# Two pre-activation 5x5 convolutions: direct products on row quads replaced by minimal F(4,3) filtering on 2x2 pixel blocks

## The chip, the cores and the metric

The kernel runs on one core of a Trainium2 chip. The core has a matrix engine (TensorE, "PE" in the profile, with "PEld" for its weight loads), three engines for elementwise work (VectorE "DVE", ScalarE "ACT", GpSimd "POOL"), and queues from which transfers between DRAM and the on-chip memories are issued; here SyncE ("SP") issues nearly all of them. On-chip data lies in SBUF, 128 partitions wide; TensorE writes its sums to PSUM, which VectorE and ScalarE read and POOL doesn't. The metric is the device time of one execution, in microseconds. The time before is the median of three runs.

## What is computed

Two layers of x = x + conv(groupnorm(x)) on an array of 8 images, 32 channels, 252 x 252 pixels, all in float32. The norm has 16 groups of two channels. The convolution is written with Fourier transforms in the reference; it comes to a 5x5 convolution with padding. The core of the reference:

```python
def conv(x, weight):                      # the same for both layers
    k = weight.shape[-1]; p = k // 2
    xp = jnp.pad(x, ((0, 0), (0, 0), (p, p), (p, p)), mode='reflect')
    ...
    wp = jnp.roll(wp, shift=(-k // 2, -k // 2), axis=(-2, -1))
    x_fft = jnp.fft.fft2(xp)
    w_fft = jnp.fft.fft2(wp)
    out_fft = jnp.einsum('bihw,oihw->bohw', x_fft, w_fft)
    out = jnp.fft.ifft2(out_fft).real
    return out[:, :, p:-p, p:-p]
...
x = x + conv(_gn(x), L0_conv_weight)
x = x + conv(_gn(x), L1_conv_weight)
```

Written out, an output pixel is a sum over 32 input channels and 5 x 5 taps of the reflected, normalised image, where the taps reach from two pixels to one side to three (after the roll) in the padded plane; the padded plane that is needed has 256 x 256 pixels, rows and columns -1 to 254.

## The kernel before

**Layout.** The 128 partitions are four quadrants of 32 channels. A quadrant holds every fourth image row, so one column position on 128 partitions is 32 channels of four neighbouring rows. An output slot is four rows; it needs two neighbouring blocks of four input rows and five column taps, so ten products of 128 x 128 matrices that are banded in (input row, output row). A product is taken for two slots at once, 2 x 252 = 504 columns; `conv` (line 201) issues the products, and an add on VectorE (line 209) puts the result on x, in place. A slot pair at the edge of a chunk splits some products in two of 252 columns.

**Stages.** An image is eight chunks of eight slots. `load` (line 67) brings a chunk of x from DRAM by four transfers, `partial_stats` (line 118) takes mean and variance of two slots at a time, `finish_stats` (lines 124 to 147) joins these, averages over the eight partitions of a group by two tiny products, and takes 1 / sqrt by a table on ScalarE and a Newton step. `normalise` (line 162) writes the normalised, shifted and padded chunk g on VectorE, and ScalarE copies edge rows and columns (lines 174 to 185). `store` (line 72) writes the result. x stays in SBUF through both layers, 18 chunk buffers for two images of eight chunks each; so each image is read once and written once.

**Order.** The program runs image after image and layer after layer; inside, chunk after chunk, each chunk's input normalised one chunk ahead of its products. The second layer of an image can't begin before the first has ended, since its norm needs the whole of the first layer's output. The code names an engine for every operation, and buffers by pools with a count of buffers (three for g, six in PSUM for products). The order on each engine's queue isn't written by hand: a planner in the framework takes the operations in an order that it works out from dependences, free buffers, the program's order and its own costs, and puts in the waits. Each engine then executes its own queue in that order.

The lines of the run that the change replaces:

```python
for b in range(B):
    for l in range(2):
        for c in range(NCH):
            ...
            for j in range(0, slots[c], 2):
                if l == 0 and b + 1 < B:
                    partial_stats(b + 1, 0, c, j)
                conv(b, l, c, j)
                if l == 0:
                    partial_stats(b, 1, c, j)
            if l == 1:
                store(b, c)
```

Of the kernel before, what the change touches and what calls it, by code (L numbers as in the profile page):

```python
# [31 lines left out]
EPS = 1e-5  # L32


@with_exitstack
def tile_conv_preact_x2(ctx: ExitStack, tc: tile.TileContext, x: bass.AP, w0: bass.AP, w1: bass.AP, out: bass.AP):
# [3 lines left out]
    assert (C, K, H % 4) == (32, 5, 0)  # L40
    NSLOT = H // 4
    CH = 8
    NCH = (NSLOT + 1) // CH
    WP = W + 4
    NPAIR = (NSLOT + 1) // 2
    slots = [min(CH, NSLOT - c * CH) for c in range(NCH)]

    const = ctx.enter_context(tc.tile_pool(name="const", bufs=1))
    xpool = ctx.enter_context(tc.tile_pool(name="xpool", bufs=2 * NCH + 2))
    gpool = ctx.enter_context(tc.tile_pool(name="gpool", bufs=3))  # L50
    small = ctx.enter_context(tc.tile_pool(name="small", bufs=3))
    ps_conv = ctx.enter_context(tc.tile_pool(name="ps_conv", bufs=6, space=bass.MemoryType.PSUM))
    ps_stat = ctx.enter_context(tc.tile_pool(name="ps_stat", bufs=2, space=bass.MemoryType.PSUM))

    quads = [slice(q * Q, (q + 1) * Q) for q in range(4)]

    def dram_rows(t: bass.AP, b: int, c: int, q: int):
        rows = t[b].rearrange("ch (t r) w -> r ch t w", r=4)
        return rows[(q - 1) % 4, :, c * CH : c * CH + slots[c], :]

# [1 line left out]
    xt = {}  # L62

    def load(b: int, c: int):
        t = xpool.tile([P, CH, W], F32, tag="x", name=f"x_{b}_{c}")
        for q in range(4):
            nc.sync.dma_start(t[quads[q], : slots[c], :], dram_rows(x, b, c, q))  # L67
        xt[b, c] = t

    def store(b: int, c: int):  # L70
        for q in range(4):
            nc.sync.dma_start(dram_rows(out, b, c, q), xt[b, c][quads[q], : slots[c], :])

    wraw = []
    for l, w in enumerate((w0, w1)):
        t = const.tile([P, K, K, C], F32, tag=f"wraw{l}", name=f"wraw{l}")
        for q in range(4):
            nc.scalar.dma_start(t[quads[q]], w)
        wraw.append(t)
    for b in range(min(2, B)):  # L80
        for c in range(NCH):
            load(b, c)

# [1 line left out]
    wt = []  # L85
    for l in range(2):
        eng = (nc.vector, nc.gpsimd)[l]
        t = const.tile([P, 2, K, 4, C], F32, tag=f"wt{l}", name=f"wt{l}")
        eng.memset(t, 0.0)
        for q in range(4):  # L90
            for blk in range(2):
                for row in range(4):
                    a = row + 4 - 4 * blk - q
                    if 0 <= a < K:
                        eng.tensor_copy(t[quads[q], blk, :, (row + 1) % 4, :], wraw[l][quads[q], a, :, :])  # L95
        wt.append(t.rearrange("p b c q o -> p b c (q o)"))

# [1 line left out]
    ident = const.tile([P, P], F32, tag="ident", name="ident")  # L99
    make_identity(nc, ident)  # L100
    member = const.tile([P, C // 2], F32, tag="member", name="member")
# [10 lines left out]
    stats, norm = {}, {}  # L112

    def partial_stats(b: int, l: int, c: int, j: int):
        if (b, l) not in stats:
            stats[b, l] = small.tile([P, NPAIR, 6], F32, tag="stats", name=f"stats_{b}_{l}")
        n = min(2, slots[c] - j)
        nc.vector.bn_stats(  # L118
            stats[b, l][:, (c * CH + j) // 2, :], xt[b, c][:, j : j + n, :].rearrange("p t w -> p (t w)")
        )  # L120

    def finish_stats(b: int, l: int):
# [24 lines left out]
        nc.vector.tensor_mul(mr[:, 1:2], inv, fix)  # L147
        norm[b, l] = mr

# [116 lines left out]
```

## Time and profile before

| What | Value |
|---|---|
| Median of three runs | 4438.5 us (4436.24 to 4440.49) |
| Span of the profiled execution | 4439.0 us |
| DMA, mean over the span | 30 GB/s, 132.59 MB |
| HBM read, written | 65.85 MB, 65.03 MB |
| VectorE busy | 1375.4 us |
| ScalarE busy | 103.1 us |
| POOL busy | 7.3 us |

The profile is of one execution, and nothing of its time lies outside its span as far as the runs can tell (4439.0 beside 4438.5). The groups of instructions give, for a line of the code and an engine, how often, how long in all, and the mean in nanoseconds; float32 products appear as two records each, and records of products in a row overlap, so the mean of a record isn't the pace. "Idle before" is the time an engine stood still in front of instructions of the group, and the arrow names what ended it.

### The profile page before, as it was taken

The page shows a single profiled execution, that of the slowest core. Times are in us where ns is not written, and L with a number is a line of the kernel's source. Part 1 is how long each engine was busy: PE and PEld are TensorE (multiplying, and loading weights), DVE is VectorE, ACT ScalarE, POOL GpSimd, SP SyncE. Part 2 cuts the span into 40 slices and gives each one's busy share as a digit, 9 for nine tenths or more (in the row PEclk, how much of TensorE's full clock was granted, in tenths as well). Part 3 has the DMA queues.
Part 4 walks back from the last instruction along what each step waited for, and adds up shares of the span by engine and source line. Part 5 has one row for each costly group of instructions (what it writes and reads, how often), then busy time and mean ns, then how long its engine had stood idle before and what let it go on. Part 6 is the DMA issues. An engine that isn't in the chain of part 4 may idle for free.

```text
span 4439.0 us, 26427 instructions
## 1 busy us (share of the span) xinstructions
PE 4296.0 (97%) x11424; PEld 2159.0 (49%) x11424; DVE 1375.4 (31%) x1726; ACT 103.1 (2%) x609; POOL 7.3 (0%) x27
## 2 busy tenths in 40 slices
PE   4999999999999999999999999999999999999999
PEld 2454445444554445444544454454445544554444
DVE  6423332332333233332333323332322332232321
ACT  0000000000000000000000000000000000000000
POOL 0000000000000000000000000000000000000000
PEclk9999999999999999999999999999999999999999
DMA  9001320023100221002210023100320001100011
GB/s 173 0 0 38 65 44 1 0 47 64 36 0 0 56 55 36 0 0 56 55 36 1 0 56 65 27 0 0 66 55 8 0 10 28 28 9 1 10 28 36
DMA packets 137716, 132.59 MB, mean 30 GB/s; under 512 B 8320, under 2 KB 137344, under 8 KB 137600
## 3 DMA queue, kind: packets, MB, share of 16 engines
q1 hardware_dynamic: 137216, 130.09, 13.9%
q8 instruction: 89, 1.46, 0.1%
q10 hardware_dynamic: 384, 0.82, 0.1%
q14 instruction: 27, 0.22, 0.0%
HBM read 65.85 MB, written 65.03 MB: 29 GB/s over the span
## 4 chain that ended last, share of the span: by engine, by line
PE 97%; DVE 2%; DMA 1%; ACT 0%; issue 0%; SPq 0%; ACTq 0%; DVEq 0%
PE ps L201 96%; DVE g L162 1%; DMA x<-in_x_dram 1%; DVE mv L124 0%; PE pv L135 0%; DVE stats L118 0%; DMA wraw<-in_L_conv_weight_dram 0%; DVE x L209 0%; PE pm L127 0%; DVE dev L130 0%; DVE sq L133 0%; DVE sq L132 0%; ACT g L182 0%; DVE mr L128 0%; SPq L67 0%
## 5 line engine op out<-in xcount | busy, mean ns | idle before, releaser
L201 PE MATMUL ps<-g,wt 128*128 128x504 f32 (+1 forms) x11360 | 4282.6, 539 | 54.4 <-ACT g L185 54.4
L201 PEld LDWEIGHTS ps<-g,wt 128*128 128x128 f32 x11360 | 2147.7, 189 | 2186.5 <-issue 2076.2
L209 DVE TENSOR_TENSOR x<-ps,x 128x504 f32<-128x504 f32 (+1 forms) x512 | 345.1, 674 | 2435.6 <-PE ps L201 2432.5
L162 DVE TENSOR_SCALAR g<-x,mr 32x1764 f32<-32x1764 f32 (+4 forms) x496 | 668.7, 1365 | 578.1 <-PE ps L201 571.8
L118 DVE BATCH_NORM_STATS2 stats<-x 128x6 f32<-128x504 f32 (+1 forms) x512 | 325.2, 669 | 26.6 <-DMA x<-in_x_dram 18.7
L182 ACT COPY g<-g 128x8 f32<-128x8 f32 x128 | 26.2, 205 | 2766.5 <-DVE g L162 2734.5
L127 PE MATMUL pm<-mv,avg 128*128 128x1 f32 x32 | 6.4, 270 | 66.5 <-DVE mv L124 66.5
L127 PEld LDWEIGHTS pm<-mv,avg 128*128 128x128 f32 x32 | 5.3, 207 | 69.6 <-DVE mv L124 69.6
L184 ACT COPY g<-g 128x8 f32<-128x8 f32 x128 | 25.6, 200 | 0.0
L185 ACT COPY g<-g 128x8 f32<-128x8 f32 x128 | 25.6, 200 | 0.0
L183 ACT COPY g<-g 128x8 f32<-128x8 f32 x128 | 25.5, 199 | 0.2
L135 PE MATMUL pv<-sq,avg 128*128 128x1 f32 x32 | 8.0, 318 | 15.2 <-DVE sq L133 15.2
L140 ACT ACTIVATE std<-var 128x1 f32<-128x1 f32 x16 | 3.2, 203 | 800.2 <-DVE var L137 800.2
L181 ACT COPY g<-row 32x252 f32<-32x252 f32 x16 | 6.4, 399 | 432.9 <-PE ps L201 432.9
L124 DVE BATCH_NORM_AGGREGATE mv<-stats 128x2 f32<-128x192 f32 x16 | 15.4, 996 | 0.3
L135 PEld LDWEIGHTS pv<-sq,avg 128*128 128x128 f32 x32 | 6.6, 257 | 16.5 <-DVE sq L133 16.5
L174 ACT COPY g<-g 32x252 f32<-32x252 f32 x16 | 6.4, 401 | 204.2 <-DVE g L162 204.2
L179 ACT COPY g<-g 32x252 f32<-32x252 f32 x16 | 6.4, 401 | 28.3 <-DVE g L162 28.3
L180 ACT COPY g<-g 32x252 f32<-32x252 f32 x16 | 6.4, 400 | 0.2
L176 ACT COPY row<-g 32x252 f32<-32x252 f32 x16 | 6.4, 397 | 0.4
L95 DVE COPY wt<-wraw 32x160 f32<-32x160 f32 x20 | 4.9, 302 | 2.6 <-DMA wraw<-in_L_conv_weight_dram 2.6
L95 POOL COPY wt<-wraw 32x160 f32<-32x160 f32 x20 | 5.5, 315 | 5.5 <-DMA wraw<-in_L_conv_weight_dram 5.3
(21 smaller groups left out, 30.6 us busy)
## 6 DMA issues: line engine op xcount, KB each, us to landing
x<-in_x_dram SPq DMA_DIRECT2D x224, 252.0 KB, 5.2
out_dram<-x SPq DMA_DIRECT2D x224, 252.0 KB, 4.2
x<-in_x_dram SPq DMA_DIRECT2D x32, 220.5 KB, 4.6
out_dram<-x SPq DMA_DIRECT2D x32, 220.5 KB, 3.5
wraw<-in_L_conv_weight_dram ACTq DMA_DIRECT2D x8, 100.0 KB, 5.1
```

The costliest lines, as they stand in the source:

```text
L95: eng.tensor_copy(t[quads[q], blk, :, (row + 1) % 4, :], wraw[l][quads[q], a, :, :])
L118: nc.vector.bn_stats(stats[b, l][:, (c * CH + j) // 2, :], xt[b, c][:, j : j + n, :].rearrange("p t w -> p (t w)"))
L124: nc.vector.bn_aggr(mv, stats.pop((b, l)).rearrange("p n s -> p (n s)"))
L127: nc.tensor.matmul(pm, avg, mv[:, 0:1], start=True, stop=True)
L135: nc.tensor.matmul(pv, avg, sq, start=True, stop=True)
L162: nc.vector.tensor_scalar(g[rows, dst, 1 : W + 1], src, mr[rows, 0:1], mr[rows, 1:2], ALU.subtract, ALU.mult)
L182: nc.scalar.copy(g[:, :, 0:1], g[:, :, 2:3])
L183: nc.scalar.copy(g[:, :, W + 1 : W + 2], g[:, :, W - 1 : W])
L184: nc.scalar.copy(g[:, :, W + 2 : W + 3], g[:, :, W - 2 : W - 1])
L185: nc.scalar.copy(g[:, :, W + 3 : W + 4], g[:, :, 3:4])
L201: nc.tensor.matmul(ps[:, at : at + m, :], wt[l][:, blk, kc, :], g[:, lo : lo + m, K - 1 - kc : K - 1 - kc + W], start=(i == 0), stop=(i == ...
L209: nc.vector.tensor_add(xs, ps[:, :n, :], xs)
```

## The change

The kernel is rewritten in its layout, its arithmetic, its storage between the layers and its order.

- **Blocks.** The partitions hold 2 x 2 pixel blocks: four quadrants for column parity and row parity. The padded plane becomes 128 x 128 blocks. A 5 x 5 kernel on pixels is a 3 x 3 kernel on blocks.
- **F(4,3) along block rows.** Four block rows of output are made from six transformed inputs instead of from 4 x 3 row taps: `transform` forms six sums v0 to v5 of input rows, `conv` multiplies each by three matrices (one per block column) for four such sets at once, 4 x 126 = 504 columns, and ten VectorE operations unite the six results into four rows. The matrices u are combinations of the kernel's rows (`make_matrices`).
- **Residual in the matrices.** x itself is no longer added: `own_pixel` adds (standard deviation) x identity, transformed in the same way, to the middle matrix of each of the six, per image and layer; the mean is added by ScalarE's copy of the first product.
- **Layer 1 through DRAM.** x isn't kept in SBUF. Its statistics are taken from a load of their own (`input_stats`), a second load brings the blocks for the convolution, layer 1's output goes to a DRAM scratch array in block layout with its padding (`to_scratch`), and layer 2 loads it from there and normalises it in place. `to_output` interleaves the columns on ScalarE and stores.
- **Normalise** is on ScalarE; the pad columns and two of the transform's subtractions are on POOL.
- **Order.** A step is a group of 16 block rows, eight per image and layer. Phases (image, layer) alternate between two images: (0,1) (1,1) (0,2) (2,1) (1,2) ... (7,1) (6,2) (7,2), counting images from 0 and layers from 1. Input statistics of the next image are taken during the phase before its first layer. Each step's input is transformed one step ahead of its products and loaded two ahead.

The core of the diff (new code; what it replaces is printed above):

```diff
+    def input_stats(b: int, c: int):
+        n = min(8, 63 - 8 * c)
+        t = spool.tile([P, 8, W], F32, tag="sx", name=f"sx_{b}_{c}")
+        rows = x[b].rearrange("ch (t r) w -> r ch t w", r=4)
+        for q in range(4):
+            nc.sync.dma_start(t[quads[q], :n], rows[q, :, 8 * c : 8 * c + n, :])
+        for j in range(0, n, 2):
+            m = min(2, n - j)
+            nc.vector.bn_stats(stat_slot(b, 0, 4 * c + j // 2), t[:, j : j + m, :].rearrange("p t w -> p (t w)"))
...
+    def own_pixel(b: int, l: int):
+        mr = norm[b, l]
+        for pc in range(2):
+            h = halves[pc]
+            nc.vector.scalar_tensor_tensor(
+                ut[l][h, :, 1 + pc, h], own[h], mr[h, 3:4], ubase[l][h], ALU.mult, ALU.add
+            )
...
+    def load(b: int, l: int, T: int):
+        nr = min(GR + 2, PB - GR * T)
+        if l:
+            g = gpool.tile([P, GR + 2, PB], F32, tag="g", name=f"g_{b}_{l}_{T}")
+            nc.sync.dma_start(g[:, :nr, :], scratch[b][:, GR * T : GR * T + nr, :])
...
+        t = xpool.tile([64, GR + 2, W], F32, tag="x", name=f"x_{b}_{T}")
...
     def normalise(b: int, l: int, T: int):
+        if T == 0:
             finish_stats(b, l)
         mr = norm[b, l]
+        nr = min(GR + 2, PB - GR * T)
+        if l:
+            g = gt[b, l, T][:, :nr, :].rearrange("p r k -> p (r k)")
+            nc.scalar.activation(g, g, AF.Identity, bias=mr[:, 2:3], scale=mr[:, 1:2])
+            return
...
+        for pc in range(2):
+            for pr in range(2):
+                q = quad(pc, pr)
+                nc.scalar.activation(
+                    g[q, :nr, 1 - pc : 1 - pc + NB],
+                    t[quads[pr], :nr, 1 - pc : W : 2],
+                    AF.Identity,
+                    bias=mr[q, 2:3],
+                    scale=mr[q, 1:2],
+                )
+        for dst, src in ((0, 1), (127, 125)):
+            nc.gpsimd.tensor_copy(g[halves[0], :nr, dst : dst + 1], g[halves[0], :nr, src : src + 1])
...
+    def transform(b: int, l: int, T: int):
...
+        nc.vector.scalar_tensor_tensor(
+            flat,
+            g[:, 0:GR, :].rearrange("p r k -> p (r k)"),
+            -4.0,
+            g[:, 2 : GR + 2, :].rearrange("p r k -> p (r k)"),
+            ALU.mult,
+            ALU.add,
+        )
+        c = apool.tile([P, NT, 2, PB], F32, tag="c", name=f"c_{n}")
+        cf = c.rearrange("p t r k -> p t (r k)")
+        nc.gpsimd.tensor_sub(cf, rows_of(g, 3), rows_of(g, 1))
+        v05 = vpool.tile([P, NT, 2, PB], F32, tag="v05", name=f"v05_{n}")
+        nc.gpsimd.tensor_sub(
+            v05.rearrange("p t r k -> p t (r k)"),
+            ab[:, :, 2:4, :].rearrange("p t r k -> p t (r k)"),
+            ab[:, :, 0:2, :].rearrange("p t r k -> p t (r k)"),
+        )
+        v = [vpool.tile([P, NT, PB], F32, tag=f"v{k}", name=f"v{k}_{n}") for k in range(1, 5)]
+        nc.vector.tensor_add(v[0], ab[:, :, 2, :], ab[:, :, 1, :])
+        nc.vector.tensor_sub(v[1], ab[:, :, 2, :], ab[:, :, 1, :])
+        nc.vector.scalar_tensor_tensor(v[2], c[:, :, 0, :], 2.0, c[:, :, 1, :], ALU.mult, ALU.add)
+        nc.vector.scalar_tensor_tensor(v[3], c[:, :, 0, :], -2.0, c[:, :, 1, :], ALU.mult, ALU.add)
...
+    def conv(b: int, l: int, T: int):
...
+        def product(f: int):
+            ps = ps_conv.tile([P, NT, NB], F32, tag="m", name=f"m{f}_{n}")
+            for b3 in range(3):
+                nc.tensor.matmul(
+                    ps,
+                    ut[l][:, f, b3, :],
+                    vs[f][:, :, 2 - b3 : 2 - b3 + NB],
+                    start=(b3 == 0),
+                    stop=(b3 == 2),
+                )
+            return ps
...
+        m1 = product(1)
+        a1 = temp("a1")
+        nc.scalar.activation(a1, m1, AF.Identity, bias=mr[:, 0:1])
+        m2 = product(2)
+        s1, d1 = temp("s1"), temp("d1")
+        v.tensor_add(s1, m2, a1)
+        v.tensor_sub(d1, a1, m2)
+        m3 = product(3)
+        a3 = temp("a3")
+        nc.scalar.copy(a3, m3)
+        m4 = product(4)
+        s2, d2 = temp("s2"), temp("d2")
+        v.tensor_add(s2, m4, a3)
+        v.tensor_sub(d2, a3, m4)
+        v.scalar_tensor_tensor(yo[1], d2, 2.0, d1, ALU.mult, ALU.add)
+        v.scalar_tensor_tensor(yo[2], s2, 4.0, s1, ALU.mult, ALU.add)
+        m0 = product(0)
+        v.tensor_add(s1, m0, s1)
+        v.tensor_add(yo[0], s1, s2)
+        m5 = product(5)
+        v.tensor_add(d1, m5, d1)
+        v.scalar_tensor_tensor(yo[3], d2, 8.0, d1, ALU.mult, ALU.add)
...
+    for i, (b, l, T) in enumerate(steps):
+        prefetch(i + 1 + AHEAD)
+        if (b, l) in before:
+            input_stats(before[b, l], T)
+        if i + 1 < len(steps):
+            normalise(*steps[i + 1])
+            transform(*steps[i + 1])
+            if steps[i + 1][2] == 0 and steps[i + 1][1] != l:
+                own_pixel(*steps[i + 1][:2])
+        conv(b, l, T)
+        if i + 1 < len(steps) and steps[i + 1][2] == 0 and steps[i + 1][1] == l:
+            own_pixel(*steps[i + 1][:2])
```

The new pools have two buffers each for the x tiles, the statistics' tiles, g, the transformed inputs v, the row tile y and the output tile o, one for the transform's intermediates (`ab`, `c`), and seven in PSUM for products.

More of the change, by code (lines that the diff above doesn't have):

```diff
@@ L32 @@
 EPS = 1e-5
+NB = 126
+PB = 128
+TR = 4
+NT = 4
+GR = TR * NT
+NG = PB // GR
+NF = 6
 @with_exitstack
@@ L39, in tile_conv_preact_x2 @@
     K = w0.shape[1]
[L40 to L46, printed above, removed]
[L48 to L50 removed]
+    assert (C, K, H, W) == (32, 5, 252, 252)
+    const = ctx.enter_context(tc.tile_pool(name="const", bufs=1))
@@ L55, in tile_conv_preact_x2 @@
+    ps_stat = ctx.enter_context(tc.tile_pool(name="ps_stat", bufs=1, space=bass.MemoryType.PSUM))
     quads = [slice(q * Q, (q + 1) * Q) for q in range(4)]
[L57 to L96, printed above, removed]
+    halves = [slice(0, 64), slice(64, 128)]
@@ new lines, in tile_conv_preact_x2, with prefetch @@
+    taps = [load_taps(0, w0)]
+    for c in range(NG):
+        input_stats(0, c)
+    make_own()
+    make_matrices(0, taps[0])
+    make_matrices(1, load_taps(1, w1))
+    phases = [(0, 0)]
+    for b in range(1, B):
+        phases += [(b, 0), (b - 1, 1)]
+    phases.append((B - 1, 1))
+    steps = [(b, l, T) for b, l in phases for T in range(NG)]
+    AHEAD = 2
+    loaded = 0
+    def prefetch(upto: int):
+        nonlocal loaded
+        while loaded < min(upto, len(steps)):
+            load(*steps[loaded])
+            loaded += 1
@@ new lines, in tile_conv_preact_x2 @@
+    prefetch(AHEAD)
+    before = {}
+    for i, (b, l) in enumerate(phases):
+        if l == 0 and i:
+            before[phases[i - 1]] = b
+    normalise(*steps[0])
+    transform(*steps[0])
+    own_pixel(*steps[0][:2])
+    for i, (b, l, T) in enumerate(steps):
[10 more added lines that the diff above has]
+            own_pixel(*steps[i + 1][:2])
```

257 lines of the change are left out of this document (174 added, 83 removed).

## The prediction

> **What bounds the kernel now.** I read the page's busy shares first, then its chain of work that ended last, then the groups of instructions.
>
> ```profile
> span 4439.0 us, 26427 instructions
> PE 4296.0 (97%) x11424; PEld 2159.0 (49%) x11424; DVE 1375.4 (31%) x1726; ACT 103.1 (2%) x609; POOL 7.3 (0%) x27
> ...
> L201 PE MATMUL ps<-g,wt 128*128 128x504 f32 (+1 forms) x11360 | 4282.6, 539 | 54.4 <-ACT g L185 54.4
> ```
>
> PE is busy for 97% of the span and stands idle in front of its products for 54.4 us in all. No other engine is busy for a third. Only fewer or faster products can shorten this, until another engine is the bound. So I need the price of a product, and then what every other engine is given per product. The trace records each float32 product twice; the pace is read from the VectorE adds that close a group of ten products (timeline of VectorE):
>
> ```profile
> 385.06 0.68 DVE L209 TENSOR_TENSOR x<-ps,x 128x504 f32<-128x504 f32 x1 [2.97 <-PE ps L201]
> 393.51 0.68 DVE L209 TENSOR_TENSOR x<-ps,x 128x504 f32<-128x504 f32 x1 [7.77 <-PE ps L201]
> ```
>
> Ten products of 504 columns take 393.51 - 385.06 = 8.45 us, 0.845 us each.
>
> **Is the order the program's?** It decides whether waits add up. Early timeline of VectorE, and a later row:
>
> ```profile
> 63.58 2.42 DVE L118 BATCH_NORM_STATS2 stats<-x 128x6 f32<-128x504 f32 x4
> 66.02 5.11 DVE L162 TENSOR_SCALAR g<-x,mr 64x2016 f32<-64x2016 f32 x4
> 71.05 0.66 DVE L209 TENSOR_TENSOR x<-ps,x 128x504 f32<-128x504 f32 x1
> ...
> 329.52 1.90 DVE L124 BATCH_NORM_AGGREGATE mv<-stats 128x2 f32<-128x192 f32 x2
> ```
>
> The program puts chunk 2's normalise (L162) behind all four adds of chunk 0; VectorE runs it ahead of the first. At 329.52 two images' statistics are closed together, though the program asks for the second one a whole convolution later. So each queue's order is a planner's, which fills idle time with later work as buffers allow. I take it to do the same with the new code.
>
> **The change, step by step.** A step is one group of 16 block rows (32 image rows) of one image and layer; there are 8 x 2 x 8 = 128.
>
> TensorE: 6 transformed inputs x 3 block columns = 18 products of 504 columns, 18 x 0.845 = 15.2 us a step, 1947 us in all, against 4282.6 now.
>
> VectorE gets most of what is added. Its prices, from the groups by form:
>
> ```profile
> L209 DVE TENSOR_TENSOR x<-ps,x 128x504 f32<-128x504 f32 x496 | 338.4, 682 | 2384.3 <-PE ps L201 2381.2
> L209 DVE TENSOR_TENSOR x<-ps,x 128x252 f32<-128x252 f32 x16 | 6.7, 420 | 51.4 <-PE ps L201 51.4
> ...
> L182 ACT COPY g<-g 128x8 f32<-128x8 f32 x128 | 26.2, 205 | 2766.5 <-DVE g L162 2734.5 <-DVE inv L142 32.0
> ...
> L174 ACT COPY g<-g 32x252 f32<-32x252 f32 x16 | 6.4, 401 | 204.2 <-DVE g L162 204.2
> L95 POOL COPY wt<-wraw 32x160 f32<-32x160 f32 x20 | 5.5, 315 | 5.5 <-DMA wraw<-in_L_conv_weight_dram 5.3
> ...
> L89 POOL MEMSET wt<- 128x1280 f32 x1 | 1.2, 1164 | 0.3 <-POOLq L253 0.3
> ```
>
> Two-input operations cost (682 - 420) / 252 = 1.04 ns per element and 0.16 us fixed. So the 2048-element row difference `ab` takes 2.29 us, the four 512-element sums v1 to v4 take 4 x 0.69 = 2.76, the ten 504-element operations that unite the products 10 x 0.682 = 6.82, and four statistics 2.42 (63.58 above). For the hand-over between dependent operations:
>
> ```profile
> 333.33 0.16 DVE L130 TENSOR_TENSOR dev<-mv,mr 128x1 f32<-128x1 f32 x1
> 333.52 0.16 DVE L132 TENSOR_TENSOR sq<-dev 128x1 f32<-128x1 f32 x1
> ```
>
> 0.19 from start to start for 0.16 of work: 0.035 x 15 = 0.5. A step is 14.8 us with statistics, 12.4 without. Of the statistics, 64 sets follow layer 1's output and 56 the inputs inside the run (8 more precede it): 128 x 12.4 + 120 x 2.42 = 1878, a mean of 14.65. That is within 4% of TensorE's 15.2: whatever lengthens VectorE's step makes it the bound.
>
> ScalarE: (401 - 205) / 244 = 0.80 ns per element and 0.2 us. Layer 1's normalise, four of 2268 elements, is 8.1 us, layer 2's in place 2.1; two PSUM copies 1.2; the four output copies of layer 2 are 4.0. At most 9.3 of 15.2 us: hidden by the products.
>
> POOL takes two subtractions of 1024 elements (`c`, `v05`) a step and, in layer 1, eight tiny edge copies. No row shows a POOL subtraction. The memset writes at 0.91 ns per element, 0.93 us for 1024; the copies go at 5.5 / 20 / 160 = 1.7 ns per element, 1.8 us, and if a second input doubles that, 3.6. I take the copy's 1.8, the row nearest in kind: 3.6 us a step, and with 0.2 for an edge copy (eight in half of the steps) 4.4 on average. The Trainium skill (GPSIMD Engine Reference, section 3.1) gives 4497 ns for an addition of 2048 elements, so 2.25 us is an estimate for each subtraction by that page; no trace here shows it, and the sum below would become 2355.
>
> POOL has room for this in 15.2 us. The open cost is whether the two engines get in each other's way. `v3` and `v4` wait for `c`, and behind them on VectorE stand all ten uniting operations, for which the PSUM buffers (7, six used per step) and hence TensorE wait. The traces show no POOL operation beside a two-input VectorE operation: the gain or loss lies between 0 and the whole 4.4. About half of VectorE's step reads PSUM or one input only (six uniting operations and the statistics, 4.1 + 2.4 of 14.8), so I let half of POOL's time fall there and charge the other half, 2.2. Step: 14.65 + 2.2 = 16.85 us.
>
> DMA. Saturated rate of loads, from the window table (engine columns, then clock, share, GB/s), and the time to landing of a store:
>
> ```profile
> 10.00:45.00 35.00, 0.00 (x0) 0.00 (x0) 18.12 (x36) 0.00 (x0) 3.29 (x12) 1.00 1.14 205
> ...
> DMA to landing us min/median/max: 2.5/3.9/5.8
> ```
>
> Layer 1 steps move 1.16 MB in and 1.05 MB out to scratch: 10.8 us at 205 GB/s. Layer 2 steps move 1.18 in, 1.03 out and 1.03 for the next image's statistics: 15.8 us, just under the step. Scratch rows are 8 KB pieces instead of 1 KB and may be faster, so this is an upper bound at full queues; I charge nothing, its cover being the 16.85 us. If steps fell to 15.2, DMA would be the bound in 48 of them.
>
> Outside the steps. Now the first product starts here:
>
> ```profile
> 49.19 1.02 DVE L124 BATCH_NORM_AGGREGATE mv<-stats 128x2 f32<-128x192 f32 x1
> ...
> 53.71 9.94 DVE L162 TENSOR_SCALAR g<-x,mr 64x2016 f32<-64x2016 f32 x7
> ...
> 59.18 71.02 PE L201 MATMUL ps<-g,wt 128*128 128x504 f32 x181 [6.90 <-ACT g L185]
> ```
>
> The same statistics, then 53.7, then 8.1 of ScalarE and 3 of the transform's first part: 65, and 11 more if the first x tiles (2.3 MB) go ahead of the last statistics. I take 72. Sixteen closings of statistics: only the six that pass from layer 2 to a new image have their last input late, with 4.5 us of closing (49.19 to 53.71), 8.1 of normalise and 3 of transform against one step of cover; 8 us each with a slow restart (below), 1 for the others: 58. The end (a sum, two copies, a store) 11. Together 141.
>
> Sum: 128 x 16.85 + 141 = 2157 + 141 = 2298, say 2300 us. The terms are of the profiled execution; its span of 4439.0 is the median of the runs, 4438.5, within 0.02%.
>
> **The rivals.**
>
> TensorE stays the bound: POOL's work falls wholly where VectorE needs one input, and the planner covers the rest. 1947 + 141 = 2088. For it: VectorE alone needs 4% less than TensorE. Against: no slack for a single late hand-over, and 15.8 us of DMA in 48 steps.
>
> POOL and VectorE exclude each other: 14.65 + 4.4 = 19.05 a step, 2438 + 141 = 2580 (with 3.6 us a subtraction, 22.65 and 3040). For it: `c` becomes ready with the same `g` as `ab`, so the two start together. Against, POOL's early copies, in windows beside VectorE's copies and after them (the fifth group of columns is POOL's):
>
> ```profile
> 7.75:9.65 1.90, 0.00 (x0) 0.00 (x0) 1.89 (x8) 0.00 (x0) 1.86 (x7) 1.00 1.10 205
> 9.65:13.40 3.75, 0.00 (x0) 0.00 (x0) 3.02 (x13) 0.00 (x0) 3.65 (x14) 1.00 1.14 202
> ```
>
> 1.86 / 7 = 0.27 us and 3.65 / 14 = 0.26: no delay, but VectorE's copies there have one input. The Trainium skill (SBUF — State Buffer, section "Who interferes with whom") has the rule: a VectorE instruction with two SBUF inputs and a POOL instruction that reads SBUF share a port as an exclusive lock for the whole instruction. By that rule the subtractions can still fall beside the PSUM operations, so it gives anything from my forecast to this rival; no run so far shows it.
>
> The queues keep the program's order. Then in the 56 steps with input statistics one chain holds everything: last sum, output copies 4.0, half a store, a load and the statistics' load queued behind it on SP (2.73 MB, 13.3 us), landing 2.5, statistics 2.42, transform 5.05, ten operations 6.82 = 34.1. The other 72 steps stay at my 16.85: 56 x 34.1 + 72 x 16.85 + 141 = 3264. Against: the order seen at 66.02 and 329.52.
>
> Slower than before: TensorE falls to half rate and stays there. After a wait of 6 us it does so for 4 us (weight loads, two per product):
>
> ```profile
> 340.52 0.50 PEld L201 LDWEIGHTS ps<-g,wt 128*128 128x128 f32 x2 [6.09 <-issue]
> ...
> 343.21 0.34 PEld L201 LDWEIGHTS ps<-g,wt 128*128 128x128 f32 x1 [0.50 <-issue]
> 344.05 0.34 PEld L201 LDWEIGHTS ps<-g,wt 128*128 128x128 f32 x1 [0.50 <-issue]
> ...
> 345.11 0.19 PEld L201 LDWEIGHTS ps<-g,wt 128*128 128x128 f32 x1 [0.24 <-issue]
> 345.53 0.19 PEld L201 LDWEIGHTS ps<-g,wt 128*128 128x128 f32 x1 [0.23 <-issue]
> ```
>
> 0.84 us between loads, then 0.42. The place is the wait for a free PSUM buffer or for `v1`. A step all at half rate takes 30.4 us; with 4 us of waits, 34.4 x 128 + 141 = 4544. It decides from (4438.5 - 141) / 128 = 33.6 us a step. Against: a slow TensorE is a busy one, and leaves no waits.
>
> **How the numbers follow.** Forecast 2300: 0.50. TensorE-bound 2088: 0.14. Exclusion 2580 and above: 0.22. Program order 3264: 0.11. Half rate 4544: 0.03. The range of 8 in 10 takes in the forecast, the TensorE bound from 2080 up, and the exclusion to 2750 (DMA waits on top); it leaves out 0.14 and the tail of the third case. A change within 0.2%, about what this measurement can tell from none, needs a coincidence: 0.005. Slower 0.03, faster 0.965.
>
> **What would show it.** TensorE: 2304 products at 0.845 us, busy 1950 us. VectorE busy 85 to 95%, its 504-element operations 0.68 us, `ab` 2.29. VectorE's idle time in front of `v3`, or longer two-input operations beside POOL, price the exclusion; POOL's groups give 1.8 or not. SP's waits in front of the statistics' loads show the program's order, weight loads 0.84 apart the half rate. Wrong would be: uniting operations that cost clearly over 0.7 us, POOL subtractions over 3 us, or a DMA share near 1 throughout layer 2's steps.

## The result, and the profile after

The changed kernel takes 3176.05 us (median of four runs, 3174.8 to 3177.34) beside 4438.39 for the kernel before: ratio 0.7155, 95% interval 0.7145 to 0.7166. It is faster, as forecast, but 876 us slower than the 2300 that was forecast, and outside the range of 2080 to 2750.

The page of the changed kernel, busy times and the slices of TensorE's and VectorE's rows:

```profile
span 3174.1 us, 17256 instructions
...
PE 2143.5 (68%) x4672; PEld 942.0 (30%) x4672; DVE 2186.5 (69%) x2701; ACT 1207.8 (38%) x866; POOL 867.1 (27%) x822
...
PE   0754868547695486954868547685486954869897
...
DVE  4766858558585585855859558585585855858686
...
PEclk9977889778897788977889778897788977889998
```

No engine is busy for more than 69%. TensorE went from 97% to 68%, and its slices rise and fall with a period of some five slices. PEclk is the clock granted to TensorE, in tenths of full speed; it falls and rises roughly with them, and its mean is 0.84, beside 0.99 in the kernel before. The groups that the prediction priced (busy time, mean ns of one, idle before them and what ended it):

```profile
L333 PE MATMUL m<-v,u 128*128 128x504 f32 x4608 | 2125.4, 624 | 878.6 <-DVE v L307 866.5 <-DVE s L363 3.9 <-DVE d L366 3.0
L299 POOL TENSOR_TENSOR c<-g 128x1024 f32<-128x1024 f32 x128 | 410.0, 3203 | 881.1 <-ACT g L259 731.8 <-DVE v L310 107.9 <-issue 32.4
L289 DVE SCALAR_TENSOR_TENSOR ab<-g 128x2048 f32<-128x2048 f32 x128 | 394.7, 3083 | 185.7 <-ACT g L259 116.4 <-POOL g L279 62.1 <-issue 5.6
L307 DVE TENSOR_TENSOR v<-ab 128x512 f32<-128x512 f32 x128 | 237.5, 1855 | 0.2
```

TensorE stands still for 878.6 us in front of its products, 866.5 of them for `v1` (L307), the first sum of the next step's transform. That one wait is as large as the whole miss, which is a likeness of size and not a sum, since the forecast too had TensorE wait for VectorE. Two rows of the waits (total, times, longest) name it, and clear the transfers:

```profile
PE m L333 <- DVE v L307: 866.5, 68, 19.8
...
DVE stats L179 <- DMA sx<-in_x_dram: 13.2, 5, 3.2
```

The timeline says why `v1` is late. A step of layer 1, VectorE first, then POOL, ScalarE and TensorE:

```profile
812.17 0.68 DVE L367 SCALAR_TENSOR_TENSOR y<-d,d 128x504 f32<-128x504 f32 x1
812.89 2.44 DVE L380 BATCH_NORM_STATS2 stats<-y 128x6 f32<-128x504 f32 x4
815.24 3.99 DVE L289 SCALAR_TENSOR_TENSOR ab<-g 128x2048 f32<-128x2048 f32 x1
819.15 0.68 DVE L309 SCALAR_TENSOR_TENSOR v<-c 128x512 f32<-128x512 f32 x1
819.75 2.82 DVE L307 TENSOR_TENSOR v<-ab 128x512 f32<-128x512 f32 x1
```
```profile
814.74 2.34 POOL L299 TENSOR_TENSOR c<-g 128x1024 f32<-128x1024 f32 x1
819.37 2.66 POOL L301 TENSOR_TENSOR v<-ab 128x1024 f32<-128x1024 f32 x1 [2.29 <-DVE ab L289]
```
```profile
804.37 9.87 ACT L269 ACTIVATE g<-x,mr 32x2268 f32<-32x2268 f32 x4
```
```profile
822.63 16.97 PE L333 MATMUL m<-v,u 128*128 128x504 f32 x36 [11.22 <-DVE v L307]
850.79 18.25 PE L333 MATMUL m<-v,u 128*128 128x504 f32 x36 [11.18 <-DVE v L307]
880.46 77.91 PE L333 MATMUL m<-v,u 128*128 128x504 f32 x180 [11.42 <-DVE v L307]
...
999.34 17.36 PE L333 MATMUL m<-v,u 128*128 128x504 f32 x36 [16.30 <-DVE v L307]
1031.79 18.20 PE L333 MATMUL m<-v,u 128*128 128x504 f32 x36 [15.09 <-DVE v L307]
```

The transform of the next step (815.24 on) stands on VectorE's queue behind the last sum of this one (812.17). TensorE, which needs that transform, has nothing to do meanwhile: 36 records (18 products), a wait of 11.2 us, 36 records again. At 880.46 five steps run in one piece, 77.91 / 5 = 15.6 us each; there the transforms stand ahead of the sums. Counted over VectorE's rows of the whole trace, the transform is late in this sense in 59 of the 127 steps that have a next one, in the later steps of every phase but the last two; in layer 2 the wait is 15 to 16 us in the rows shown (999.34 on). From product to product a late step takes 850.79 - 822.63 = 28.2 us in layer 1 and 1031.79 - 999.34 = 32.5 in layer 2. Added up over the trace, TensorE's waits in front of the 59 steps that follow are 802.6 us, 13.6 each. (The 14.7 us in an expectation below are 866.5 / 59 and so count in 19.8 us in front of the first product and some 44 elsewhere.)

The products behind such a wait also begin slowly: the granted clock is 0.51 from 850.79 to 856.50 and 1.00 from there to 868.00. The 59 steps that follow a late transform take 17.8 us on average, where 36 records that run on take 15.4.

### The profile page after: what moved, and what is told of

The parts are those of the page before. It is cut to its first block, busy times and chain, and to the rows that moved or that the text cites. A ratio compares the mean times of both kernels' runs of the same rounds, so it can differ in the third digit from the quotient of the medians.

```text
span 3174.1 us, 17256 instructions
## 1 busy us (share of the span) xinstructions
PE 2143.5 (68%) x4672; PEld 942.0 (30%) x4672; DVE 2186.5 (69%) x2701; ACT 1207.8 (38%) x866; POOL 867.1 (27%) x822
## 5 line engine op out<-in xcount | busy, mean ns | idle before, releaser
L333 PE MATMUL m<-v,u 128*128 128x504 f32 x4608 | 2125.4, 624 | 878.6 <-DVE v L307 866.5
L333 PEld LDWEIGHTS m<-v,u 128*128 128x128 f32 x4608 | 926.3, 203 | 2070.4 <-issue 1144.5
L299 POOL TENSOR_TENSOR c<-g 128x1024 f32<-128x1024 f32 x128 | 410.0, 3203 | 881.1 <-ACT g L259 731.8
L269 ACT ACTIVATE g<-x,mr 32x2268 f32<-32x2268 f32 (+1 forms) x256 | 617.7, 2413 | 5.8 <-DVE mr L208 1.2
L289 DVE SCALAR_TENSOR_TENSOR ab<-g 128x2048 f32<-128x2048 f32 x128 | 394.7, 3083 | 185.7 <-ACT g L259 116.4
L412 ACT COPY o<-y 64x1008 f32<-64x1008 f32 (+1 forms) x256 | 277.6, 1084 | 505.8 <-DVE y L367 335.7
L301 POOL TENSOR_TENSOR v<-ab 128x1024 f32<-128x1024 f32 x128 | 323.6, 2528 | 221.4 <-DVE ab L289 142.4
L351 DVE TENSOR_TENSOR s<-m,a 128x504 f32<-128x504 f32 x128 | 86.5, 676 | 323.0 <-PE m L333 260.2
L358 DVE TENSOR_TENSOR s<-m,a 128x504 f32<-128x504 f32 x128 | 86.7, 678 | 250.7 <-PE m L333 207.8
L307 DVE TENSOR_TENSOR v<-ab 128x512 f32<-128x512 f32 x128 | 237.5, 1855 | 0.2
L309 DVE SCALAR_TENSOR_TENSOR v<-c 128x512 f32<-128x512 f32 x128 | 168.3, 1315 | 83.0 <-POOL c L299 83.0
L179 DVE BATCH_NORM_STATS2 stats<-sx 128x6 f32<-128x504 f32 (+1 forms) x256 | 153.4, 658 | 13.2 <-DMA sx<-in_x_dram 13.2
L308 DVE TENSOR_TENSOR v<-ab 128x512 f32<-128x512 f32 x128 | 104.1, 813 | 0.0
```

What stands on the lines that cost most here:

```text
L179: nc.vector.bn_stats(stat_slot(b, 0, 4 * c + j // 2), t[:, j : j + m, :].rearrange("p t w -> p (t w)"))
L269: nc.scalar.activation(g[q, :nr, 1 - pc : 1 - pc + NB], t[quads[pr], :nr, 1 - pc : W : 2], AF.Identity, bias=mr[q, 2:3], scale=mr[q, 1:2],)
L289: nc.vector.scalar_tensor_tensor(flat, g[:, 0:GR, :].rearrange("p r k -> p (r k)"), -4.0, g[:, 2 : GR + 2, :].rearrange("p r k -> p (r k)" ...
L299: nc.gpsimd.tensor_sub(cf, rows_of(g, 3), rows_of(g, 1))
L301: nc.gpsimd.tensor_sub(v05.rearrange("p t r k -> p t (r k)"), ab[:, :, 2:4, :].rearrange("p t r k -> p t (r k)"), ab[:, :, 0:2, :].rearran ...
L307: nc.vector.tensor_add(v[0], ab[:, :, 2, :], ab[:, :, 1, :])
```

## The experiments

Theory: the order that the planner gives the queues costs the time. Rivals: the lock between VectorE and POOL (`ab` took 3.99 us above, `v1` 2.82); the transfers; later, SyncE's order and a second queue. All ratios are to the kernel before, with 95% intervals.

**Pin VectorE's and ScalarE's queues to the program's order.** In the program, each transform stands ahead of the sums.

```diff
+    E = mybir.EngineType
+    ctx.enter_context(tc.manual_schedule(engines={E.DVE, E.Activation}))
```

> The changed kernel with VectorE's and ScalarE's queues kept in the order of the program text (the planner still orders SP, POOL and TensorE); nothing else differs. Order theory: the 59 steps whose transform stands behind the former step's sums in VectorE's queue vanish, TensorE's 866 us of waits for v1 fall below 300, steps of layer 1 come to about 18 us and of layer 2 to about 21 (output copies, normalise, transform and sums in one chain), about 2640 us in all. Lock theory (VectorE and POOL shutting each other out is what makes steps long): the operations are the same, so 3000 us or more. Transfer theory (loads land late): no change, about 3170.

3154.71 us, 0.7105 (0.7095 to 0.7116). The theory in this form falls: no transform is late, next to nothing is won, and TensorE still waits 711.0 us for `v1`. A wait has moved to VectorE. SyncE's rows of one layer 2 step stand below it:

```profile
DVE stats L181 <- DMA sx<-in_x_dram: 388.8, 39, 20.5
...
1048.41 3.09 SPq L419 DMA_DIRECT2D out_dram<-o  x4
1051.54 8.37 SPq L178 DMA_DIRECT2D sx<-in_x_dram  x7
```

The program's order puts the statistics ahead of the next transform on VectorE. On SyncE, whose queue the planner still orders, their load (1051.54) is issued behind the output's stores (1048.41), which wait for ScalarE's output copies. VectorE stood 388.8 us in front of statistics that waited 13.2 us before.

**Pin every queue to the program's order.**

```diff
+    ctx.enter_context(tc.manual_schedule())
```

> All five queues in the order of the program text. This is the prediction's rival of program order: in the 56 steps with input statistics, last sum, output copies, half a store, a load, the statistics' load, statistics, transform and sums make one chain of about 34 us, the other steps 17 to 21: about 3260 us. If SP's queue isn't what holds (order theory alone, VectorE and ScalarE pinned suffice), it equals the run with only these two pinned, about 2640. Transfer theory: above 3170, since loads are issued no earlier than now.

3639.25 us, 0.8198 (0.8185 to 0.8212), with 1009.8 us of the same wait. So the planner was worth 463 us against the order as written.

**Both subtractions on VectorE, in the planner's order.**

```diff
-        nc.gpsimd.tensor_sub(cf, rows_of(g, 3), rows_of(g, 1))
+        nc.vector.tensor_sub(cf, rows_of(g, 3), rows_of(g, 1))
...
-        nc.gpsimd.tensor_sub(
+        nc.vector.tensor_sub(
             v05.rearrange("p t r k -> p t (r k)"),
```

> The two subtractions of POOL (c and v05) are moved to VectorE; the planner's order is free and still has 59 steps with the transform behind the sums. Lock theory: ab returns to 2.29 us, v1 to 0.69, v3 to 0.69, 3.0 us a step less on VectorE against 2.4 more for the subtractions, and the way to v1 shortens by the whole excess in all 128 steps: 2790 us or less. Order theory: the 59 serial steps stay, each shorter by 2 to 4 us on the way to v1: 2900 to 3040. Transfer theory: about 3170.

2899.31 us, 0.653 (0.652 to 0.654): 277 less. VectorE does more and is busy for less (2070.4 against 2186.5 us), and 59 transforms are still late. TensorE's wait for `v1` is 644.6 us in place of 866.5. The lock is real, but it isn't the larger part, and the 277 us aren't its price alone: the planner forms `v1` ahead of `v3` in all 128 steps here, while the changed kernel forms `v3` first in 83, the 59 late ones among them.

**A hand-made order, same operations and engines.** All queues pinned; loads three steps ahead and ahead of the stores, statistics' loads before they are wanted, the output copies of a step behind the second next normalise (with three buffers for g and one for the temporaries).

```diff
+    ctx.enter_context(tc.manual_schedule())
...
         if (b, l) in before:
-            input_stats(before[b, l], T)
+            stat_take(before[b, l], T)
         if i + 1 < len(steps):
             normalise(*steps[i + 1])
+            prefetch(i + 1 + AHEAD)
+            for o in outs:
+                to_output(*o)
+            outs.clear()
             transform(*steps[i + 1])
...
         conv(b, l, T)
+        stat_prefetch(i + 1)
```

> All queues pinned, with the program text itself rearranged: loads are issued three steps ahead and in front of the step's stores, statistics' loads two steps ahead, the output copies of a step stand behind the next normalise, g has three buffers and the temporaries of the sums one. Order theory: no chain is left, and VectorE's 17.1 us of work a step (with the lock's 3.0) is the bound: 128 x 17.3 + 141 = 2355 us. Lock theory: the lock's cost stays and grows with the overlap, 2600 or more. Transfer theory: 15.8 us a step of layer 2 at 205 GB/s binds together with late landings, 2600 or more.

2451.41 us, 0.5521 (0.5512 to 0.5529). The same operations and bytes, pinned in different orders, span 2451 to 3639 us: order decides. The changed buffers don't explain it, since the late orders below have this run's buffers too and take 2744 to 3101 us. VectorE still has the lock in it:

```profile
PE 2039.2 (83%) x4672; PEld 899.3 (37%) x4672; DVE 2206.2 (90%) x2701; ACT 1209.9 (49%) x866; POOL 810.7 (33%) x822
```

**Which part of the order?** Three runs undo it piece by piece, the first two in the same 59 steps, the third in all.

```diff
+            if i not in LATE:
                 transform(*steps[i + 1])
...
         conv(b, l, T)
+        if i in LATE:
+            transform(*steps[i + 1])
```

> The hand-made order of reorder_all (2451 us), but in the 59 steps where the planner placed it so, the next step's transform (VectorE's and POOL's part) stands behind the last sum; the queues of ScalarE and SyncE keep reorder_all's order. So this prices the place of the transform on VectorE's queue by itself. Order theory: PE stands still from its last product over the last sum, two of the transform's operations and the lock, 11.2 us in the timeline of the changed kernel's layer-1 steps: 2451 + 59 x 11 = about 3100 us, and PE's waits for v1 at 650 us. Rival, SyncE's chain (stores ahead of the loads hold everything, and the transform's place only follows): under 2650 us, since the loads come early here.

2743.68 us, 0.618 (0.617 to 0.619): 292 more, 5 us a late step, less than half of what was expected. The rows show what is missing:

```profile
552.40 17.15 PE L346 MATMUL m<-v,u 128*128 128x504 f32 x36 [4.42 <-DVE v L320]
...
703.65 18.32 PE L346 MATMUL m<-v,u 128*128 128x504 f32 x36 [7.63 <-DVE v L320]
```

Where TensorE waits for `v1` here, it waits 4.4 to 9.4 us in layer 2 and 7.6 in layer 1 (where 2.4 of statistics come between), not 16 and 11: g lies ready, and POOL, which stood idle for 15.6 us ahead of `v05` at 551.77, has long done `c`. Next, ScalarE's normalise is put behind the output copies too, as the planner has it:

```diff
         conv(b, l, T)
+        if late:
+            put = [out_copies(*o) for o in outs]
+            outs.clear()
+            normalise(*steps[i + 1])
+            prefetch(i + 1 + AHEAD)
+            for p in put:
+                out_stores(*p)
+            transform(*steps[i + 1])
```

> late_transform (2744 us), and in the same 59 steps ScalarE's part is late too, as the planner has it: the next step's normalise stands behind the products' copies and, in layer 2, behind the output copies. The loads stay ahead of the stores on SyncE's queue. If the places on VectorE's and ScalarE's queues together make the changed kernel's time: 3050 to 3200 us, with waits of PE for the transform of 11 us in layer 1 and 15 in layer 2, 59 x 12.5 = 740 above reorder_all's 2451. If SyncE's order (stores ahead of loads) makes the rest: under 2900.

3007.34 us, 0.6776 (0.6766 to 0.6786): 264 more, below the 3050 expected. Last, the order within the transform, changed in all 128 steps (the changed kernel has `v3` first in 83):

```diff
+        nc.vector.scalar_tensor_tensor(v[2], c[:, :, 0, :], 2.0, c[:, :, 1, :], ALU.mult, ALU.add)
         nc.vector.tensor_add(v[0], ab[:, :, 2, :], ab[:, :, 1, :])
         nc.vector.tensor_sub(v[1], ab[:, :, 2, :], ab[:, :, 1, :])
-        nc.vector.scalar_tensor_tensor(v[2], c[:, :, 0, :], 2.0, c[:, :, 1, :], ALU.mult, ALU.add)
```

> late_normalise_transform (3007 us) with one line moved: v3 is formed ahead of v1 on VectorE, as the planner has it in the changed kernel. There v1, for which TensorE waits, then starts 0.6 us later and meets POOL's second subtraction: 2.82 us in place of 0.69 in the timeline, so TensorE waits 11.2 us in a layer-1 step where late_normalise_transform has 8.6. If this is what is left of the difference to the changed kernel: 59 x 2.65 = 156 us more, 3140 to 3190. If SyncE's order (stores ahead of loads) makes the rest: 3000 to 3030.

3100.57 us, 0.6982 (0.6969 to 0.6994): 93 more, not the 156 expected. Most late steps now wait as in the changed kernel:

```profile
825.50 16.87 PE L346 MATMUL m<-v,u 128*128 128x504 f32 x36 [11.21 <-DVE v L321]
...
1803.50 17.67 PE L346 MATMUL m<-v,u 128*128 128x504 f32 x36 [16.25 <-DVE v L321]
```

11.21 us beside 11.22 in layer 1, 16.25 beside 15.09 to 16.30 in layer 2. Of the 725 us between the hand-made order and the changed kernel, undone in this sequence, 292 are the transform's place on VectorE's queue, 264 the normalise's on ScalarE's (loads and stores moved with it), 93 `v1` behind `v3` and POOL; 76 stay unexplained, SyncE's order (stores ahead of loads) among the candidates.

**Why does the planner put them late?** Only the queue that issues some transfers is changed; the planner orders the rest.

```diff
-            nc.sync.dma_start(t[quads[q], :n], rows[q, :, 8 * c : 8 * c + n, :])
+            nc.gpsimd.dma_start(t[quads[q], :n], rows[q, :, 8 * c : 8 * c + n, :])
```

> Only the queue from which the loads for the input statistics are issued is changed (POOL's in place of SyncE's); the order stays the planner's. In the changed kernel 59 of 128 steps have the next step's transform placed behind the last sum on VectorE's queue; here 20 have it, since the planner no longer counts these loads against the one queue. Planner theory (the planner prices the transfers of one queue one after another and, taking them for the bound, doesn't hurry the transform): each such step costs PE about 866.5 / 59 = 14.7 us of waiting for v1, so 39 fewer of them save about 500 to 570 us: 2610 to 2680 us, and PE's waits for v1 fall to about 300 us. Transfer theory (bytes or SBUF room bound it): the bytes are the same, about 3170. Lock theory (VectorE and POOL hinder each other and that alone makes the waits): unchanged or worse, 3150 or more, since POOL now has 224 issues more to do.

2935.74 us, 0.6613 (0.6602 to 0.6624). The count of 20 in this expectation was wrong: the trace has 54 late steps, so the time expected of it doesn't follow. They lie elsewhere: all 25 of layer 2 (32.5 us in the rows above) are gone, and layer 1 has 54 in place of 34 (28.2 us in the rows above). The order moved with the queue, though no engine's work changed.

```diff
-                    nc.sync.dma_start(
+                    nc.scalar.dma_start(
                         sc[q, to * PB : (to + n) * PB], y[q, pc + first * PB : pc + (first + n) * PB]
...
-                nc.sync.dma_start(dst[1 - pr, :, first : first + n, :], o[quads[2 * s + pr], :n, :])
+                nc.scalar.dma_start(dst[1 - pr, :, first : first + n, :], o[quads[2 * s + pr], :n, :])
```

> Only the queue of the large stores (to scratch and to the output) is changed, ScalarE's in place of SyncE's; the order stays the planner's. Two of 128 steps are left with the next transform behind the last sum. Planner theory: 57 x 14 us less than 3176, about 2380 to 2480 us; VectorE at 17.1 us a step (with its lengthened operations) becomes the bound. Transfer theory: about 3170. Rival, the new wait: ScalarE stands in front of each store for the sums of the step, and the next step's normalise and PSUM copies are queued behind it, 2700 to 3000.

2558.91 us, 0.5764 (0.5755 to 0.5772): two lines take 617 us away, and two late steps are left of 59. It lies between the 2380 to 2480 of the planner theory and the 2700 to 3000 of the rival in the expectation. TensorE still waits for `v1` at fewer places, and what holds `v1` there wasn't followed further:

```profile
PE m L333 <- DVE v L307: 374.5, 37, 19.8
```

With both subtractions on VectorE as well:

> Stores from ScalarE's queue as in the run beside it, and the two subtractions of the transform on VectorE in place of POOL; three steps are left with the transform behind the last sum. VectorE was busy for 2070 us with the subtractions on it and the old order, 16.2 us a step, against 2186 with them on POOL. If what is left after the order is mended is VectorE's work with the lock in it: 128 x 16.2 + 141 = 2215 to 2350 us, some 120 under the run beside it. If the lock costs only where the transform is on the path, the two are alike within 40 us.

2410.73 us, 0.5431 (0.5423 to 0.5439): 148 us less, but 2215 to 2350 isn't reached. Here too the planner forms `v1` first in all steps, where it had `v3` first in 56.

Is it the second queue itself? Both moves again, with the late order pinned (late_normalise_transform, 3007 us):

> late_normalise_transform (3007 us) with the large stores issued from ScalarE's queue, as in stores_act_queue (2559 us, against 3176 with the planner's order on one queue), but with the late order kept. If a second queue is of use by itself (transfers no longer stand behind each other), some hundred us go: 2500 to 2850. If it helped there only since the planner then laid the order out differently: 2980 to 3120, the upper part if ScalarE's standing in front of the stores delays the next normalise.

3583.78 us, 0.8073 (0.8059 to 0.8088). Far above what either side expected: ScalarE stands in front of the stores for the step's sums, and the next normalise behind them: in layer 1 it waits 382.6 us there, ended by the stores to scratch, which late_normalise_transform doesn't show. So this says nothing of the queue alone. The loads for the statistics need no such wait:

> late_normalise_transform (3007 us) with the loads for the input statistics issued from POOL's queue, as in stat_loads_pool_queue (2936 us against 3176 with the planner's order on one queue), and the late order kept. late_stores_act (3584 us) couldn't tell the second queue's own worth, since ScalarE stood in front of the stores; here POOL issues loads whose buffers are free, so it needn't stand. If a second queue is of use by itself: 2770 to 2900. If it helps only through the order that the planner then makes: 2980 to 3060.

3029.18 us, 0.6827 (0.6816 to 0.6839), 22 more than on one queue. In this order the second queue by itself gains nothing, so for the statistics' loads the 240 us are put down to the order that the planner made. For the stores the same is likely (two late steps instead of 59) but the control that was to show it brought a wait of its own. That the planner prices one queue's transfers as if one came after the other, and so takes the queue for the bound, fits the runs in which it orders the queues; its costs stand in no trace, so this is inferred.

**A better version.** The hand-made order with the subtractions on VectorE:

> The hand-made order of reorder_all (2451 us) with the two subtractions on VectorE in place of POOL. VectorE was busy for 2206 us of 2449 there; without the lock it should be 2070, and the time 2300 to 2330 us. If the lock costs nothing off the path: 2440 to 2460. If VectorE's own longer row of operations ahead of v1 delays PE more than the lock does: above 2460.

2336.58 us, 0.5263 (0.5255 to 0.5271): 115 less, near the 2300 to 2330 expected. Both runs have the same order of operations, so this is the lock's price less that of the work added to VectorE. Then the closings of the statistics, in front of which TensorE stood 241.7 us, were moved (statistics one step earlier, the small products inside the last but one step's products):

```diff
         v.tensor_sub(d1, a1, m2)
+        if close:
+            close_b(*close)
...
         m0 = product(0)
+        if close:
+            close_c(*close)
...
+        close = phases[i // NG + 1] if T == NG - 2 and i + 2 < len(steps) else None
+        if close:
+            close_a(*close)
-        conv(b, l, T)
+        conv(b, l, T, close)
```

> reorder_subs_dve (2337 us), with the input statistics taken one step earlier and the closing of the next phase's statistics placed inside the products of the step before the last, in place of behind them. PE waited there for 241.7 us in front of the 16 closings, 71.6 of them at the start. If these waits are what the phase changes cost, some 130 to 170 us go and PE's own 15.2 to 15.8 us a step becomes the bound: 2170 to 2220 us. If the wait only moves on (to v1 of the next phase, or to its middle matrices): above 2280.

2358.52 us, 0.5312 (0.5304 to 0.5319): 22 slower. The wait had only moved. TensorE, in front of the mean's small product:

```profile
648.44 0.59 PE L206 MATMUL pm<-mv,avg 128*128 128x1 f32 x2 [13.36 <-DVE mv L198]
```

VectorE is a whole transform behind TensorE here, and TensorE has to let it catch up. So one step more, with the statistics two steps earlier and their joining ahead of a transform:

```diff
         v.tensor_sub(d1, a1, m2)
-        if close:
-            close_b(*close)
+        if close and T == NG - 2:
+            close_c(*close)
...
         v.scalar_tensor_tensor(yo[3], d2, 8.0, d1, ALU.mult, ALU.add)
+        if close and T == NG - 3:
+            close_b(*close)
```

> early_closing moved the closing ahead by less than VectorE's backlog: TensorE came to the mean's small product 13.4 us before VectorE had reached the joining of the statistics. Here the input statistics are taken two steps earlier, the joining is ahead of the transform in the third step from the end, the first small product behind that step's six products and the second in the next step. If the backlog was the wait, PE's waits in front of the closings fall from 257 us to the 70 at the start and below 40 for the other 15, and the time is 2130 to 2220 us. If VectorE itself is the bound (2071 us busy of 2337), the wait moves to v1: above 2280.

2247.84 us, 0.5064 (0.5056 to 0.5073), the fastest here, though 28 above the 2130 to 2220 expected. Page and waits:

```profile
PE 2023.4 (90%) x4672; PEld 893.6 (40%) x4672; DVE 2071.1 (92%) x2957; ACT 1212.1 (54%) x866; POOL 117.4 (5%) x566
```
```profile
PE pm L206 <- DVE mv L198: 71.0, 1, 71.0
```

Of TensorE's waits for the means (256.6 us in early_closing) only the start's is left, and VectorE is busy for 92% and TensorE for 90% of the span.

## Why the prediction went wrong, point by point

- **The step that failed** is "Is the order the program's?", with its end "I take it to do the same with the new code". The planner hoists in the kernel before, where transfers fill little of the time (30 GB/s), and the rows quoted there are true; with the new code it left 59 of the transforms behind the sums. Waits that the forecast covered by hoisting came back: 866.5 us for `v1`. With an order that does hoist (and a third buffer for g), the forecast's own operations take 2451 us, inside the range.
- **The program-order rival**, 3264, came near the time by another mechanism. It put the loss into the 56 steps with input statistics, behind stores and loads on SyncE (8 of them are in layer 1 and have no output copies, which its sum overlooks). In the changed kernel that load is waited for 13.2 us in all, and 34 of the 59 late steps are in layer 1. The rival's own mechanism is what pin_all shows: 1009.8 us of that wait, and 3639.
- **TensorE**, 18 x 0.845 = 15.2 us a step, was right: 15.48 us for 36 records that run on in early_closing, 15.6 above. Busy time is 2125 us instead of 1950 since products after a wait begin slowly: 16.97 to 18.25 us for the same 36 records behind 11 us of standing still. The sign of the half-rate rival is there, weight loads 0.84 us apart (851.79 to 855.99), but for 3 to 6 us behind a wait and not for a whole step.
- **VectorE**, 14.65 us a step, was 6% high. With the subtractions on it, reorder_subs_dve has 2076.2 us, 311.7 of them for the subtractions: 1764.5 / 128 = 13.8, the start included. Operations that don't wait for each other begin 0.59 us apart, not 0.68 + 0.035 (VectorE's timeline of early_closing, with `ab` and `v1` undisturbed ahead of them):

```profile
624.55 2.27 DVE L315 SCALAR_TENSOR_TENSOR ab<-g 128x2048 f32<-128x2048 f32 x1
...
629.01 0.68 DVE L333 TENSOR_TENSOR v<-ab 128x512 f32<-128x512 f32 x1
...
631.42 0.67 DVE L377 TENSOR_TENSOR s<-m,a 128x504 f32<-128x504 f32 x1
632.01 0.67 DVE L378 TENSOR_TENSOR d<-a,m 128x504 f32<-128x504 f32 x1
632.60 0.67 DVE L386 TENSOR_TENSOR s<-m,a 128x504 f32<-128x504 f32 x1
```

- **ScalarE**, taken as hidden by the products, needs 9.87 us and not 8.1 for layer 1's normalise (804.37), and its late place on the queue cost 264 us in late_normalise_transform.
- **POOL's subtraction**, 1.8 us from the copies, was 2.34 where nothing disturbed it (814.74). The Trainium skill's figure in GPSIMD Engine Reference, section 3.1, gave an estimate of 2.25, and the trace agrees within 4%.
- **The exclusion** exists, and costs more than was charged: VectorE's 2186.5 us are 17.1 a step, 3.3 above its own 13.8, where 2.2 was charged on 14.65. That 17.1 is so near the forecast's 16.85 is luck, since the two misses cancel. In the forecast it was a wait in front of `v3`; it showed as longer operations, `ab` and `v1` above all. That is the Trainium skill's rule in SBUF — State Buffer, section "Who interferes with whom": whichever issues first has the shared ports for its whole instruction, and the other is blocked until then. The trace agrees within 0.15 us: `ab`, issued at 815.24, can begin when `c` ends at 817.08 and takes its 2.27 from there, 819.35 against 819.23; `v1`, issued 0.38 behind `v05`, ends at 822.57, 0.54 behind `v05`'s end. At 881.53 `ab` comes first and takes 2.28 us, and `c`, issued 0.31 behind it, takes 4.18.
- **DMA** at no charge was right: no large wait names a transfer, and the fastest version moves the same bytes in 2245 us.
- **Outside the steps**, 141: the first product starts at 84.57, not 72, and the 58 for phase changes were too little, hidden by the larger miss. In reorder_subs_dve the closings behind the first cost 241.7 - 71.6 = 170 us. The forecast gave six closings a price and ten almost none; the fifteen cost 11 us each on average (2.4 to 16.8), since VectorE comes to them a transform late.

## What to carry to other kernels

When a planner or a compiler orders the queues, the order is a term of the prediction: read it, step by step, in the new code's own queues, and don't carry it over from another kernel. A period in the slices of every engine, with none of them full, was its mark here; the wait in front of TensorE, which the forecast had near its limit, then named the operation that stood too late. Where two engines work one step apart, place a small joint operation (a closing of statistics) by the later engine's position, not by the program's.

## What was not expected of the hardware

- TensorE restarts slowly: in the changed kernel, all 64 steps behind the first that follow a wait of over 4 us take 16.9 to 18.5 us, where a step that runs on takes 15.4, and the granted clock is 0.50 to 0.54 for the first 3 to 6 us (822.63, 850.79, 880.46, 1066.07). A wait of 11 us costs some 2 us more than it lasts. The prediction shows it behind one wait (340.52); here it comes behind every long one.
- A VectorE operation with two inputs in SBUF that meets a POOL subtraction grows by what is left of that subtraction: `v1` from 0.68 to 2.82 us, `ab` from 2.27 to 3.99. Doing the two subtractions on VectorE, 1.22 us each in reorder_subs_dve (311.7 / 256), in place of POOL's 2.34 was faster in all three pairs tried, by 277, 148 and 115 us; only in the last pair is the order of operations the same.
